# Column sums of a softmax taken through HBM and VectorE in place of products with ones, and one image's projection begun a unit sooner

## The chip, the cores and the metric

One NeuronCore of a Trainium2 chip runs the whole program. Its engines work side by side and wait for one another through semaphores: TensorE (PE, matrix products, with PEld its weight loads), VectorE (DVE), ScalarE (ACT), GpSimd (POOL) and SyncE (SP). SP and POOL also issue the DMAs, each from a queue of its own that is worked in order; 16 DMA engines carry out what both queues ask for. The time is that of the device in microseconds (us), as the median of several runs. The profile is of one execution of its own.

## What is computed

Self-attention over four images of 64 x 64 positions with 256 channels, in float32. Cut to what matters:

```python
def _L0_conv_ref(x, Wq, bq, Wk, bk, Wv, bv, gamma):
    B, W, H, C = x.shape                    # 4, 64, 64, 256
    N = W * H                               # 4096
    q = jnp.einsum('bwhc,cd->bwhd', x, Wq) + bq      # d = 128
    k = jnp.einsum('bwhc,cd->bwhd', x, Wk) + bk
    v = jnp.einsum('bwhc,cd->bwhd', x, Wv) + bv      # d = 256
    pq = q.reshape(B, -1, N)
    pk = k.reshape(B, -1, N)
    pv = v.reshape(B, -1, N)
    energy = jnp.einsum('bcn,bcm->bnm', pq, pk)
    attention = jax.nn.softmax(energy, axis=-1)
    out = jnp.einsum('bcm,bnm->bcn', pv, attention)
    out = out.reshape(B, W, H, C)
    return gamma * out + x
```

The inputs are seeded normal numbers; `gamma` is 0.5.

## The kernel before

**Tiles and units.** The energy is never stored. For each image the 4096 columns n are cut into 8 groups of 512 (`NB`), and the 4096 rows m into 16 units of 256 (two blocks of 128 rows). A unit makes exp(energy) of 256 x 512 elements as a tile `x` of 128 partitions x 2 x 512, and adds its products with `v` to four PSUM banks (`a0`, `b0`, `a1`, `b1`) that gather over the group. There are 4 x 8 x 16 = 512 units, numbered n; t = n % 16 is a unit's place in its group, and the loop over n is written out by hand (from line 706). Nothing but this order, the semaphores and the numbers of buffers sets what runs when.

**Two parts for each number.** Products run in a faster format with fewer bits, so each operand is split into an upper part `h` and two residues `l` and `d`, and each product is three products. Per unit PE does `cross` (L365, two products), `attend` for the first half of the channels (L437, six), `energy` (L380, four) and `attend` for the second half (six). `cross` and `energy` work two units ahead (`LOOK`). ACT does the exponentials (L383), the upper parts (L389) and the scaling of energies (L366). DVE does, in `halves(n + 1)`, three operations on 1024 elements for each unit: the running sum `s` (L400) and the two residues (L414, L416) into a tile `ld` with two buffers.

**The projection of the next image** (q, k, v from x) is cut into 16 steps for each pair of column blocks and slipped into the units by `step(p, engine)`: eight transposes in one step, products in six, and on DVE one or two operations of 512 elements in most (L164, L284, L309). Its results go to HBM through SP (`kf`, `qd`, `vf` stores, L337), and come back through POOL when they are needed: `load_k` in each unit, into three buffers and three units ahead; `load_q` once a group; `load_v` in the units t = 3 to 15 of an image's last group and t = 0 to 2 of the next image. The projection of image 0 runs ahead of the loop, alone.

**The column sums.** After a group, `s` (128 x 2 x 512) holds for each partition the sums over the group's units; the softmax needs the sum over all partitions and both halves, for each of the 512 columns. The kernel before does this so:

- in `halves` of the group's last unit the two halves of `s` are added (L406, `whole`);
- `sum_forms` splits the 512 columns into an upper part (ACT, L464) and a residue (DVE, L466), which are put into a `q` tile that is free at that time;
- `sums` multiplies both with a 128 x 128 matrix of ones on PE (L476), which leaves the total of each column in each partition, and ACT copies one row of it back to `s` (L477);
- `finish` is a chain of pieces, one per unit: the row goes to HBM (`zd`, L484), comes back as 128 x 4 (L486), its reciprocal is taken (L489), goes to HBM again (`rd`, L491), comes back spread over all partitions (L495), and the group's output `o` is multiplied with it (L498). Then POOL adds the input image to `o` in a DMA that accumulates (L502), and SP stores the result (L506).

`finish` begins in the unit t = 0 after the group (t = 2 in the last image), right behind `sums`. A piece runs at the end of each unit (`proceed`). The two halves of the output that were gathered in `a` and `b` are moved into `o` by `emptied` (L455, L457) at t = 15 and in the first units of the next group, and added in `finish` (L492).

The last group of all does not use `finish` but `finish_last`, which is not touched.

Of the kernel before, what the change touches and what calls it, by code (L numbers as in the profile page):

```python
# [9 lines left out]
F32 = mybir.dt.float32  # L10
F32R = mybir.dt.float32r
I32 = mybir.dt.int32
AF = mybir.ActivationFunctionType
ALU = mybir.AluOpType
AX = mybir.AxisListType
# [5 lines left out]
def kernel(  # L21
# [36 lines left out]
    nc = tc.nc  # L58
    B, W, H, C = x.shape
    P = 128  # L60
# [19 lines left out]
    UPPER = 1.0 - 2.0**-13  # L80
    REST = 1.0 / (1.0 + E)
    NB = 512
    NJ = NB // P
    NG = N // NB
    NU = NM // 2
    STEPS = NG * NU
# [4 lines left out]
    ones_r = const.tile([P, P], F32R, name="ones")  # L91
# [9 lines left out]
    with ExitStack() as fast:  # L101
        fast.enter_context(tc.manual_schedule())
        pool = lambda name, bufs, **kw: fast.enter_context(
            tc.tile_pool(name=name, bufs=bufs, **kw)
        )
        qkv = pool("qkv", 1)
        ppool = pool("ppool", 2)
        work = pool("work", 2)
        kpool = pool("kpool", 3)
        dram = pool("dram", 2, space=DRAM)  # L110
        ps_e = pool("ps_e", 2, space=PSUM)
        ps_p = pool("ps_p", 1, space=PSUM)
        ps_o = pool("ps_o", 1, space=PSUM)
# [1 line left out]

        vall = qkv.tile([P, NU, 2, 3, C], F32R, tag="v", name="v")
        wf = qkv.tile([P, 2, 3, KC, C], F32R, tag="wf", name="wf")
        zd, rd = (dram.tile([B * NG, NB], F32, tag=n, name=n, bufs=1) for n in ("zd", "rd"))
        xs4 = work.tile([P, 4, 2, XB], F32, tag="o", name="xs", bufs=1)
        raw = ppool.tile([P, 2, KC, C], F32, tag="x", name="raw")  # L120
        scaled = ppool.tile([P, 2, KC, C], F32, tag="x", name="scaled")
# [22 lines left out]
        qd, kf, vf, units, loads, now = {}, {}, {}, {}, {}, {}  # L144
        active, stores = [], []
# [49 lines left out]
        def spare(name, shape):  # L195
            pool, tag = now["banks"][now["turn"] % len(now["banks"])]
            return pool.tile(shape, F32, tag=tag, name=name)
# [142 lines left out]
        def load_v(b, t):  # L340
            for i in range(2):
                nc.gpsimd.dma_start(vall[:, t, i], vf[b, t][:, i])

        def load_q(b, g):
            loads["q", b, g] = qs[g % 2]
            nc.gpsimd.dma_start(loads["q", b, g], qd[b, g])

        def load_k(n):
# [43 lines left out]
        def halves(n):  # L392
            if n >= B * STEPS:
                return
            x, h = units[n]

            def summed():
                if n % NU:
                    s = now["s"]
                    nc.vector.tensor_tensor(s, s, x, ALU.add)  # L400
                else:
                    now["s"] = x

            def whole():
                s = now["sum"] = now["s"]
                nc.vector.tensor_tensor(s[:, 0, :], s[:, 0, :], s[:, 1, :], ALU.add)  # L406

            if n not in (1, 2):
                summed()
            if n == B * STEPS - 1:  # L410
                whole()
            ld = ppool.tile([P, 2, 2, NB], F32R, tag="ld", name=f"ld_{n}")
            l, d = ld[:, 0], ld[:, 1]
            nc.vector.tensor_tensor(l, x, h.bitcast(F32), ALU.subtract)  # L414

            nc.vector.scalar_tensor_tensor(  # L416
                d, h.bitcast(F32), 1.0 + E, x, ALU.mult, ALU.subtract
            )
            if n in (1, 2):
                summed()  # L420
            if n % NU == NU - 1 and n < B * STEPS - 1:
                whole()
            units[n] = h, l, d

        def attend(n, j, order=(0, 1, 2)):
# [30 lines left out]
                    else:  # L456
                        nc.scalar.activation(to, y, AF.Identity, scale=scale)  # L457

        def sum_forms(n):

            s = now["total"] = now["sum"]
            f = qs[n // NU % 2].rearrange("p j f a -> p (j f a)")
            h, l = now["z"] = f[:, :NB], f[:, NB : 2 * NB]
            nc.scalar.activation(h, s[:, 0, :], AF.Identity, scale=UPPER)  # L464
            yield
            nc.vector.tensor_tensor(l, s[:, 0, :], h.bitcast(F32), ALU.subtract)  # L466
            yield

        def sums(n):
            if n + NU < (B - 1) * STEPS:  # L470
                zp = spare(f"z_{n // NU}", [P, NB])
            else:
                pool, tag = (ps_o, "b1") if n // NU % 2 else now["banks"][1]
                zp = pool.tile([P, NB], F32, tag=tag, name=f"z_{n // NU}")
            for f, x in enumerate(now["z"]):
                nc.tensor.matmul(zp, ones_r, x, start=(f == 0), stop=(f == 1))  # L476
            nc.scalar.copy(now["total"][0:1, 0, :], zp[0:1, :])  # L477

        def finish(n, o, s):
            b, g = divmod(n, NG)  # L480
            r4 = rall[:, n, :]
            row = lambda t: t[n : n + 1, :]
            spread = lambda t: row(t).rearrange("o (p j) -> (o p) j", j=NJ)
            nc.sync.dma_start(row(zd), s[0:1, 0, :])  # L484
            yield
            nc.sync.dma_start(r4, spread(zd))  # L486
            yield
            yield
            nc.vector.reciprocal(r4, r4)  # L489
            yield  # L490
            nc.sync.dma_start(spread(rd), r4)  # L491
            nc.vector.tensor_tensor(o[:, 0], o[:, 0], o[:, 1], ALU.add)  # L492
            yield
            r = o[:, 1, 0]
            nc.sync.dma_start(r, rd[n, :].partition_broadcast(P))  # L495
            yield
            yield
            nc.vector.tensor_tensor(  # L498
                o[:, 0], o[:, 0], r.unsqueeze(1).to_broadcast([P, 2, NB]), ALU.mult
            )  # L500
            yield
            nc.gpsimd.dma_start(o[:, 0], xg[b, g], accum_op=ALU.add)  # L502
            yield
            yield
            yield
            nc.sync.dma_start(og[b, g], o[:, 0])  # L506

        def inside(ok, r):
# [114 lines left out]
        now["turn"], now["banks"] = 0, [(ps_p, "p0"), (ps_p, "p1")]  # L623
        rings = cycle(now["banks"]), cycle([(ps_o, tag) for tag in ("a0", "b0", "a1", "b1")])
        image(0)
        qs = [work.tile([P, NJ, 3, P], F32R, tag=f"q{g}", name=f"q{g}", bufs=1) for g in range(2)]
        loads["q", 0, 0] = qs[0]
        f3 = qs[1].rearrange("p (s w) f a -> p s w f a", s=2)
        for i in range(4):
            load_x(0, i)  # L630
        transposed(0, 0)
# [26 lines left out]
        for i in range(NI):  # L658
# [21 lines left out]
            vs = v_forms(i)  # L680
# [25 lines left out]
        for n in range(B * STEPS):  # L706
            b, u = divmod(n, STEPS)
            g, t = divmod(u, NU)
            final = n == B * STEPS - 1
            if n == 0:  # L710
                image(1)
                load_x(1, 0)
            if u == STEPS - 5 and b + 2 < B:
                image(b + 2)
            if n == B * STEPS - 6:
                xr = ppool.tile([P, 2, NB], F32, tag="s", name="xr")
                nc.sync.dma_start(xr, xg[b, g])
            cross(n + LOOK)
            turn = t == NU - 1 and not final
            if t == 0 and n:  # L720
                upper(n + LOOK - 1)
            if turn:
                zf = sum_forms(n)
                next(zf)
            p = n - 3 + (n > 6) + (n > 17)
            step(p, "act")
            late = n >= (B - 1) * STEPS
            if not final:
                attend(n, 0)
            if late and 1 <= t <= 2 and n > 1:  # L730
                emptied(n - 1 - t, 1, done, t - 1)
            energy(n + LOOK)
            load_k(n + LOOK + 3)
            store()
            if t == 0 and n:
                done = full
            if turn:
                emptied(n, 0)
            else:
                upper(n + LOOK)  # L740
            step(p, "pe")
            if t == 2 * late and n > 2:
                sums(n - 1 - 2 * late)
                active.append(finish(n // NU - 1, now["o"], now["total"]))
            if t == 0 and n and not late:
                emptied(n - 1, 1, done, vector=True)
            halves(n + 1)
            if n == 0:
                next(vs)
                next(vs, None)  # L750
            if turn:
                next(zf)
            step(p, "dve")
            if final:
                finish_last(n, xr)
                break
            attend(n, 1)
            full = now["a", 1], now["b", 1]
            if n in (6, 17):
                for engine in ("act", "pe", "dve"):  # L760
                    step(p + 1, engine)
            if t == 6 and n + NU < B * STEPS:
                load_q(*divmod(n // NU + 1, NG))
            if n >= STEPS - NU + 3 and (n - 3) // NU % NG == NG - 1 and (n - 3) // STEPS + 1 < B:
                load_v((n - 3) // STEPS + 1, (n - 3) % NU)
            proceed()

    NB = 512
    NG = N // NB
    NJ = NB // P  # L770
    NP = NM // 2
    with tc.If(nc.values_load(again[0:1, 0:1]) > 0), ExitStack() as general:
        pool = lambda name, bufs, **kw: general.enter_context(
            tc.tile_pool(name=name, bufs=bufs, **kw)
        )
        xpool, xtpool, qkv = pool("gx", 2), pool("gxt", 2), pool("gqkv", 1)
        ppool, work = pool("gp", NP + 2), pool("gw", 1)
# [13 lines left out]
        ps_o = pool("go", 1, space=PSUM)  # L791
# [72 lines left out]
        for b in range(B):  # L864
# [16 lines left out]
            for g in range(NG):  # L881
                ps = []
                mx = work.tile([P, 2, NB], F32, tag="mx", name=f"gmx_{b}_{g}")
                for t in range(NP):
                    sp = ps_s.tile([P, 2, NB], F32, tag="s", name=f"gs_{b}_{g}_{t}")
                    for h in range(2):
# [4 lines left out]
                            start=True,  # L891
                            stop=True,
# [91 lines left out]
```

## Time and profile before

| | us |
|---|---|
| median of 3 runs | 2339.01 (2337.47 to 2340.04) |
| the profiled execution's own time | 2337.63 |
| its span, first to last instruction | 2335.85 |
| mean granted TensorE clock | 0.999 of full |

| group of instructions | count | mean ns | busy us |
|---|---|---|---|
| PE products of `attend`, L437 | 6144 | 390 | 634.7, 631.9 and 631.9 for the three parts |
| PE products of the energy, L380 and L365 | 3072 | 390 | 548.2 and 316.1 |
| PE products with ones, L476 | 62 | 403 | 19.9 |
| DVE running sum, L400 | 480 | 1223 | 587.1 |
| DVE residues, L414 and L416 (without a group's first unit) | 960 | 1221 | 586.7 and 585.8 |
| DVE L406 and L466 | 32 and 31 | 685 and 684 | 21.9 and 21.2 |
| ACT L464 and L477 | 31 and 31 | 621 and 557 | 19.3 and 17.3 |

A mean is an instruction's own length in the record. Neighbouring products overlap (a product of 512 columns begins 0.227 us after the one before it), and neighbouring DVE operations by some 0.09 us, so counts times means come to more than the busy time. The DMA engines move 412.9 MB in all, 177 GB/s on the mean.

A view that tells much here is the same busy times in equal stretches. Columns: stretch and length in us, then for PE, PEld, DVE, ACT and POOL the busy us and in brackets the instructions, then the granted clock, the share of the DMA engines and GB/s. One stretch is about one group:

```profile
775.00:846.10 71.10, 71.10 (x330) 59.41 (x329) 67.02 (x67) 55.61 (x90) 9.64 (x18) 1.00 0.58 166
...
1201.60:1272.70 71.10, 71.10 (x330) 59.37 (x329) 66.66 (x68) 55.94 (x91) 18.66 (x34) 1.00 0.88 284
...
1983.70:2054.80 71.10, 71.10 (x315) 58.86 (x314) 62.86 (x58) 57.02 (x93) 10.65 (x19) 1.00 0.49 134
```

The first is an ordinary group with projection, the second one at the boundary of two images, where the next image's v is loaded, the third one of the last image, which has no projection beside it.

### The profile page before, as it was taken

How to read it: one execution, taken by the hardware profiler on the slowest of the kernel's cores; microseconds unless marked ns; L12 is line 12 of the kernel's file. 1: busy time of each engine (PE TensorE's matmuls, PEld its weight loads, DVE VectorE, ACT ScalarE, POOL GpSimd, SP SyncE). 2: the span in 40 equal slices, each digit the busy share in tenths (PEclk: the TensorE clock that was granted, in tenths of full speed). 3: DMA queues.
4: the chain of work that ended last, by engine and by line, in shares of the span. 5: the costliest groups of instructions: out<-in, count | busy, mean ns of one | idle time of the engine just before them, and what ended most of it. 6: DMA issues, size and time to landing. Idle time of an engine off the chain costs nothing.

```text
span 2335.8 us, 31727 instructions
## 1 busy us (share of the span) xinstructions
PE 2325.0 (100%) x10820; PEld 1944.9 (83%) x10820; DVE 2151.9 (92%) x2144; ACT 1829.1 (78%) x2980; POOL 416.2 (18%) x716
## 2 busy tenths in 40 slices
PE   9999999999999999999999999999999999999998
PEld 9888888888888888888888888888888888888887
DVE  8999999999999999999999999999999888888888
ACT  7778777787777877778777778777787788888886
POOL 7111111111321111111132111111113111111110
PEclk9999999999999999999999999999999999999999
DMA  8555655566985666555697556655569644444453
GB/s 271 154 173 167 183 173 152 156 174 183 297 245 152 177 177 173 164 148 171 180 326 234 144 180 168 188 159 153 167 178 342 171 135 123 122 131 114 134 134 97
DMA packets 192075, 412.90 MB, mean 177 GB/s; under 512 B 27521, under 2 KB 77443, under 8 KB 191906
## 3 DMA queue, kind: packets, MB, share of 16 engines
q0 software_dynamic: 101120, 280.54, 44.5%
q1 hardware_dynamic: 90238, 129.99, 15.9%
q8 instruction: 89, 1.46, 0.3%
q14 instruction: 80, 0.66, 0.1%
q10 hardware_dynamic: 548, 0.26, 0.0%
HBM read 305.73 MB, written 104.20 MB: 175 GB/s over the span
## 4 chain that ended last, share of the span: by engine, by line
PE 99%; DVE 1%; DMA 0%; issue 0%; ACT 0%; DVEq 0%
PE a L437 40%; PE b L437 20%; PE e L380 20%; PE e L365 10%; PE qv L256 5%; PE v L273 3%; PE xt L218 1%; PE z L476 1%; DMA xs<-in_x_dram 0%; DVE ld L414 0%; DVE ld L416 0%; DVE v L164 0%; DVE f L309 0%; DVE q L309 0%; DVE s L400 0%
## 5 line engine op out<-in xcount | busy, mean ns | idle before, releaser
L383 ACT ACTIVATE x<-e 128x512 f32<-128x512 f32 x960 | 522.0, 596 | 308.5 <-PE e L380 308.5
L400 DVE TENSOR_TENSOR s<-s,x 128x1024 f32<-128x1024 f32 x480 | 587.1, 1223 | 78.5 <-ACT x L383 76.3
L366 ACT ACTIVATE e<-e 128x512 f32<-128x512 f32 x1024 | 546.8, 572 | 132.7 <-PE e L365 132.7
L414 DVE TENSOR_TENSOR ld<-x,h 128x1024 fp32r<-128x1024 f32 x480 | 586.7, 1222 | 58.7 <-PE b L437 40.8
L437 PE MATMUL a<-h,v 128*128 128x512 f32 x2048 | 634.7, 391 | 0.0
L437 PE MATMUL b<-ld,v 128*128 128x512 f32 x2048 | 631.9, 390 | 0.6 <-DVE ld L416 0.6
L437 PE MATMUL a<-ld,v 128*128 128x512 f32 x2048 | 631.9, 390 | 0.0
L352 POOL DMA_DIRECT2D k<-kf x512 | 272.5, 532 | 1868.4 <-PE e L380 1736.3
L416 DVE SCALAR_TENSOR_TENSOR ld<-h,x 128x1024 fp32r<-128x1024 f32 x480 | 585.8, 1220 | 0.0
L380 PE MATMUL e<-q,k 128*128 128x512 f32 x2048 | 548.2, 390 | 0.0
L389 ACT ACTIVATE h<-x 128x1024 fp32r<-128x1024 f32 x480 | 510.6, 1064 | 14.2
L437 PEld LDWEIGHTS b<-ld,v 128*128 128x128 f32 x2048 | 384.4, 188 | 81.9 <-DVE ld L416 2.0
L437 PEld LDWEIGHTS a<-ld,v 128*128 128x128 f32 x2048 | 384.6, 188 | 80.9
L380 PEld LDWEIGHTS e<-q,k 128*128 128x128 f32 x2048 | 384.5, 188 | 79.5
L437 PEld LDWEIGHTS a<-h,v 128*128 128x128 f32 x2048 | 379.9, 188 | 74.9
L365 PE MATMUL e<-q,k 128*128 128x512 f32 x1024 | 316.1, 390 | 0.0
L365 PEld LDWEIGHTS e<-q,k 128*128 128x128 f32 x1024 | 192.0, 188 | 40.1
L309 DVE SCALAR_TENSOR_TENSOR f<-f,qv 128x512 fp32r<-128x512 f32 x118 | 79.5, 681 | 0.3
L256 PE MATMUL qv<-wf,xf 128*128 128x256 f32 x576 | 77.2, 285 | 0.7 <-DVE qv L284 0.4
L256 PEld LDWEIGHTS qv<-wf,xf 128*128 128x128 f32 x576 | 73.8, 191 | 3.8 <-DVE qv L284 0.6
L164 DVE SCALAR_TENSOR_TENSOR vf<-vf,v 128x512 fp32r<-128x512 f32 x96 | 65.4, 682 | 0.6 <-ACT vf L154 0.6
L414 DVE TENSOR_TENSOR ld<-s,h 128x1024 fp32r<-128x1024 f32 x32 | 39.2, 1226 | 28.7 <-ACT h L389 27.2
(95 smaller groups left out, 1166.4 us busy)
## 6 DMA issues: line engine op xcount, KB each, us to landing
k<-kf POOLq DMA_DIRECT2D x512, 384.0 KB, 3.4
vf<-vf SPq DMA_DIRECT2D x96, 384.0 KB
v<-vf POOLq DMA_DIRECT2D x96, 384.0 KB, 7.0
q<-qd POOLq DMA_DIRECT2D x31, 768.0 KB, 5.1
kf<-f SPq DMA_DIRECT2D x118, 192.0 KB
qd<-f SPq DMA_DIRECT2D x115, 192.0 KB
o<-in_x_dram POOLq DMA_DIRECT2D x31, 512.0 KB, 6.7
out_dram<-o SPq DMA_DIRECT2D x31, 512.0 KB
```

The lines of the kernel that those rows point to most:

```text
L256: nc.tensor.matmul(to[:, s, :], left, right.rearrange("p s a -> p (s a)") if w else right, start=(f == 2 and s == k == 0), stop=(f == 1 an ...
L309: nc.vector.scalar_tensor_tensor(f[:, :, :, j, :], h.bitcast(F32), s, y, ALU.mult, op)
L352: nc.gpsimd.dma_start(t, kf[b, u % NU])
L365: nc.tensor.matmul(e, *forms(n, i, 2), start=True, stop=False, skip_group_check=True)
L366: nc.scalar.mul(e, e, -REST)
L380: nc.tensor.matmul(e, *forms(n, i, f), start=False, stop=(f == 1), skip_group_check=True)
L383: nc.scalar.activation(x[:, i, :], e, AF.Exp, scale=(1.0 + E) ** 3 / E)
L389: nc.scalar.activation(h, units[n], AF.Identity, scale=UPPER)
L400: nc.vector.tensor_tensor(s, s, x, ALU.add)
L414: nc.vector.tensor_tensor(l, x, h.bitcast(F32), ALU.subtract)
L416: nc.vector.scalar_tensor_tensor(d, h.bitcast(F32), 1.0 + E, x, ALU.mult, ALU.subtract)
L437: nc.tensor.matmul(to, vall[:, t, i, f, j * P : (j + 1) * P], units[n][f][:, i, :], start=(t == 0 and i == 0 and f != 1), stop=(t == NU - ...
```

## The change

The products with ones, the split in front of them and the copy behind them go. `finish` now begins in the unit t = 15 itself. It stores both halves of `s` whole (128 x 512 each) to HBM, and eight DMAs read them back so that partition 32 j + p holds, for the 128 columns of block j, eight values of each column: from partitions p, p + 32, p + 64, p + 96 of both halves. DVE adds these eight (one reduction with 1024 inputs and 128 results), transposes the result in blocks of 32 x 32, and adds over the 32 that now lie side by side (a reduction of 128 to 4). That leaves the totals as 128 x 4, as they were before. The tile `y` that is read into takes the place of the `q` tile of the group just done; `load_q` of the group after next therefore comes at t = 8, no longer at t = 6. The pieces of `finish` now fall in the units: zd stores t = 15, y loads 0, sum of the halves of `o` 3, reductions, reciprocal and rd store 6, spread read 7, multiplication 9, accumulation 10, output store 13.

Image 1's projection begins in unit 2 instead of 3, and the unit 6 does one of its steps instead of two. In units 1 to 4 the running sum is added behind the residues, not ahead of them (before: units 1 and 2), and the last forms of image 0's v, which stood in unit 0, are made behind the residues of unit 2.

```diff
-        zd, rd = (dram.tile([B * NG, NB], F32, tag=n, name=n, bufs=1) for n in ("zd", "rd"))
+        zd = dram.tile([B * NG, 2, P, NB], F32, tag="zd", name="zd", bufs=1)
+        rd = dram.tile([B * NG, NB], F32, tag="rd", name="rd", bufs=1)
...
+        def q_tile(g, name, dtype=F32R):
+            return work.tile([P, NJ, 3, P], dtype, tag=f"q{g % 2}", name=name, bufs=1)
+
         def load_q(b, g):
-            loads["q", b, g] = qs[g % 2]
+            loads["q", b, g] = q_tile(g, f"q_{b}_{g}")
             nc.gpsimd.dma_start(loads["q", b, g], qd[b, g])
...
-            if n not in (1, 2):
+            after = 0 < n < 5
+            if not after:
                 summed()
...
-            if n in (1, 2):
+            if n == 2:
+                next(vs)
+                next(vs, None)
+            if after:
                 summed()
-            if n % NU == NU - 1 and n < B * STEPS - 1:
-                whole()
             units[n] = h, l, d
...
-        def sum_forms(n):
-            s = now["total"] = now["sum"]
-            f = qs[n // NU % 2].rearrange("p j f a -> p (j f a)")
-            h, l = now["z"] = f[:, :NB], f[:, NB : 2 * NB]
-            nc.scalar.activation(h, s[:, 0, :], AF.Identity, scale=UPPER)
-            yield
-            nc.vector.tensor_tensor(l, s[:, 0, :], h.bitcast(F32), ALU.subtract)
-            yield
-
-        def sums(n):
...
-            for f, x in enumerate(now["z"]):
-                nc.tensor.matmul(zp, ones_r, x, start=(f == 0), stop=(f == 1))
-            nc.scalar.copy(now["total"][0:1, 0, :], zp[0:1, :])
-
         def finish(n, o, s):
             b, g = divmod(n, NG)
             r4 = rall[:, n, :]
-            row = lambda t: t[n : n + 1, :]
-            spread = lambda t: row(t).rearrange("o (p j) -> (o p) j", j=NJ)
-            nc.sync.dma_start(row(zd), s[0:1, 0, :])
+            for i in range(2):
+                nc.sync.dma_start(zd[n, i], s[:, i, :])
             yield
-            nc.sync.dma_start(r4, spread(zd))
-            yield
-            yield
+            y = q_tile(n, f"y_{n}", F32).rearrange("p j f a -> p (j f) a")
+            for j in range(NJ):
+                for i in range(2):
+                    nc.sync.dma_start(
+                        y[j * 32 : (j + 1) * 32, NJ * i : NJ * (i + 1)],
+                        zd[n, i].rearrange("(a p) (j c) -> j p a c", p=32, j=NJ)[j],
+                    )
+            for _ in range(3):
+                yield
+            nc.vector.tensor_tensor(o[:, 0], o[:, 0], o[:, 1], ALU.add)
+            for _ in range(3):
+                yield
+            nc.vector.tensor_reduce(
+                y[:, 8].rearrange("p (f c) -> p c f", f=NJ),
+                y[:, :8].rearrange("p a (c f) -> p c f a", f=NJ),
+                AX.X,
+                ALU.add,
+            )
+            nc.vector.transpose(y[:, 9], y[:, 8])
+            nc.vector.tensor_reduce(r4, y[:, 9].rearrange("p (f c) -> p f c", f=NJ), AX.X, ALU.add)
             nc.vector.reciprocal(r4, r4)
-            yield
-            nc.sync.dma_start(spread(rd), r4)
-            nc.vector.tensor_tensor(o[:, 0], o[:, 0], o[:, 1], ALU.add)
+            nc.sync.dma_start(rd[n, :].rearrange("(p j) -> p j", j=NJ), r4)
             yield
...
-            p = n - 3 + (n > 6) + (n > 17)
+            p = n - 2 + (n > 17)
             step(p, "act")
...
-            if t == 2 * late and n > 2:
-                sums(n - 1 - 2 * late)
-                active.append(finish(n // NU - 1, now["o"], now["total"]))
+            if turn:
+                active.append(finish(n // NU, now["o"], now["s"]))
...
-            if n in (6, 17):
+            if n == 17:
                 for engine in ("act", "pe", "dve"):
                     step(p + 1, engine)
-            if t == 6 and n + NU < B * STEPS:
+            if t == 8 and n + NU < B * STEPS:
                 load_q(*divmod(n // NU + 1, NG))
```

## The prediction

> **What bounds the kernel now.** I read the page first: busy shares and the chain of waits.
>
> ```profile
> PE 2325.0 (100%) x10820; PEld 1944.9 (83%) x10820; DVE 2151.9 (92%) x2144; ACT 1829.1 (78%) x2980; POOL 416.2 (18%) x716
> ...
> PE 99%; DVE 1%; DMA 0%; issue 0%; ACT 0%; DVEq 0%
> ```
>
> TensorE (PE) is the chain; VectorE (DVE) is close behind. "100% busy" can hide pauses, since matmul records overlap, so I took the distance between starts from the timeline. Around the first product of ones (L476):
>
> ```profile
> 139.70 1.08 PE L380 MATMUL e<-q,k 128*128 128x512 f32 x4
> ...
> 140.61 0.64 PE L476 MATMUL z<-q,ones 128*128 128x512 f32 x2
> ...
> 141.09 0.63 PE L437 MATMUL a<-h,v 128*128 128x512 f32 x2
> ```
>
> Four L380 products fill 0.91 us (0.227 each), the pair L476 0.48, and the next product follows at once. So each L476 pair is paid in full, with no wait before it. Two places where PE does wait lie in the first units, for L416's second residue:
>
> ```profile
> 73.92 0.61 PE L437 MATMUL a<-ld,v 128*128 128x512 f32 x2
> 74.77 0.72 PE L437 MATMUL b<-ld,v 128*128 128x512 f32 x2 [0.23 <-DVE ld L416]
> ...
> 78.55 0.61 PE L437 MATMUL a<-ld,v 128*128 128x512 f32 x2
> 79.50 0.73 PE L437 MATMUL b<-ld,v 128*128 128x512 f32 x2 [0.34 <-DVE ld L416]
> ```
>
> Two products take 0.45, but here 0.85 and 0.95 pass between the starts, and about 0.1 more behind each: 1.1 us in all.
>
> Next, how much room DVE has where the new reduction goes (unit t=6 of a group), from DVE's timeline and PE's:
>
> ```profile
> 241.23 1.22 DVE L400 TENSOR_TENSOR s<-s,x 128x1024 f32<-128x1024 f32 x1
> 242.36 1.23 DVE L414 TENSOR_TENSOR ld<-x,h 128x1024 fp32r<-128x1024 f32 x1
> 243.50 1.23 DVE L416 SCALAR_TENSOR_TENSOR ld<-h,x 128x1024 fp32r<-128x1024 f32 x1
> ...
> 248.58 0.62 PE L437 MATMUL b<-ld,v 128*128 128x512 f32 x2
> ```
>
> The residue is ready at 244.73 and read at 248.58: 3.85 us of room. (1024 elements cost DVE 1.14 us from start to start.)
>
> Last, the DMA engines. Where the next image's v is loaded beside everything else (units t=3 of an image's last group to t=2 of the next image), the windows show:
>
> ```profile
> 1187.00:1191.00 4.00, 4.00 (x19) 3.29 (x18) 3.46 (x4) 2.39 (x5) 0.10 (x1) 1.00 0.84 264
> 1191.00:1195.00 4.00, 4.00 (x20) 3.30 (x19) 3.69 (x4) 3.55 (x7) 2.61 (x5) 1.00 0.82 216
> ...
> 1207.00:1211.00 4.00, 4.00 (x19) 3.34 (x18) 3.64 (x4) 3.28 (x6) 1.60 (x3) 1.00 1.12 388
> ...
> 1215.00:1219.00 4.00, 4.00 (x19) 3.31 (x18) 3.56 (x4) 3.25 (x6) 0.90 (x2) 1.00 1.14 380
> ```
>
> The last two columns are DMA share and GB/s: full from 1199 to 1239. A k load normally lands 3.4 us after its issue (page, part 6); here
>
> ```profile
> 1227.72 0.53 POOL L342 DMA_DIRECT2D v<-vf  x1 [0.39 <-DMA k<-kf]
> ...
> 1227.68 0.63 PE L365 MATMUL e<-q,k 128*128 128x512 f32 x2
> ```
>
> the k load issued at 1218.10 lands 9.34 us later, at 1227.44, and L365 reads it at 1227.68: 0.24 us of room. At the other two image boundaries (633 to 656 and 1787 to 1804) the least room, found the same way, is 1.36 and 1.38 us. Elsewhere it is 4 us and more.
>
> **The change, part by part.** Sums are against the profiled execution, 2337.63 us (span 2335.85 and 1.8 around it); the median of the runs is 2339.01, 1.4 above.
>
> (1) L476 goes, 31 pairs. Pair 0.481 (from 140.61 to 141.09), and 0.006 more for the L380 product in front, which then follows at the usual 0.227: 31 x 0.487 = -15.1 us. Nothing is put on PE.
>
> (2) Image 1's projection starts at unit 2, not 3, and the double step at unit 6 goes; the sum s is added behind the residues in units 1 to 4, and image 0's last v forms (two L164, 1.2 us) move from unit 0 to behind unit 2's residue. The late residue of unit 2 was 0.5 us late: 1.2 earlier, it is in time. Unit 3's was 0.6 late: one sum (1.14) goes from in front of it, and the eight transposes (0.9 us on PE, needed anyway) come before it. Bounds: both waits stay (0), both go (-1.1). I take -1.1.
>
> (3) Off DVE: L406 and L466, 0.69 and 0.68; off ACT: L464 and L477, 0.62 and 0.56. Both lie beside PE: 0. New on DVE: a reduction of 1024 elements, a transpose of 128x128, a reduction of 128, behind them the reciprocal. The last two have rows (L542 0.29, L489 0.17); the transpose is nearest to L510 (128x128, 0.23). The big reduction reads with a step of 512 bytes, which no row shows: at best the 1.22 of a contiguous one (L400), at worst the slowest elementwise row, POOL's L160, 1.30 for 512 elements, 2.6 for 1024. Chain: 1.9 to 3.3 us. I take 1.9, since DVE itself shows 1.22 for every 1024-element form. Room in units 7 and 8 of images 0 to 2 is 3.85, and the multiplication L498 leaves (it moves to t=9). In the last image the residue is ready 2.44 before its reader (1981.91 against 1984.35) and DVE idles 0.58 a unit: 3.0 of room. So 0; at 3.3, 8 x 0.3 = 2.4 us. Without this cover each group would pay the chain. L492 moves from t=4 to t=3: 1.14 us, one unit earlier, and the 1.4 us of room that unit 6 has today is what units 5 and 6 then have: 0.
>
> (4) DMAs on SP, per group: one row of 2 KB out and 2 KB back become 0.52 MB out (two stores) and 0.52 MB back (eight loads that wait for them). At t=15 and t=0 SP has only the vf stores and the x loads; behind the waiting loads stand one group's last vf stores at most, wanted seven units later. In ordinary groups DMA is at a share of 0.6 and k has 4 us: 0. On POOL, load_q moves from t=6 to t=8, the accumulation (L502) from t=8 to t=10; on SP the output store from t=11 to t=13, behind the x loads. At the three image boundaries this falls into the full stretch. Before the tightest k load come 0.52 MB of zd stores, and the 0.79 MB of load_q, issued at 1180.4 ahead of the slack stretch 1187 to 1195, now come at its end. At 387 GB/s that is 1.35 + 2.05 = 3.4 us; the stretch 1191 to 1195 can absorb (1 - 0.82/1.13) x 4 = 1.1. So the load is 2.3 to 3.4 us later, against room of 0.24, 1.36 and 1.38: PE waits 2.1 to 3.2, 0.9 to 2.0 and 0.9 to 2.0, 3.9 to 7.2 us in all. What is late next is the loop itself, so a wait is paid once per boundary. I take 5.5. Bounds: 0 if the queues' order favours k; with the 0.52 MB of y loads as well (1.35 x 3) and the output store late for L457 at t=15, 11.4.
>
> Sum: -15.1 - 1.1 + 5.5 = -10.7 us: 2326.9 for an execution like the profiled one, 2328.3 as a median.
>
> **The rivals.** (B) The transfers are hidden after all: -16.2, median 2322.8. For it: POOL's queue held 70% of the engines' time against SP's 43% from 1203 to 1223, so k is not starved. Against it: 0.24 us of room.
>
> (C) Slower: the strided reduction is the new bound, in each group at t=6. Decisive point: beyond 3.85 us of chain (23 finishes in images 0 to 2) and 3.0 (8 in the last) PE waits for the residue. 23 x (X - 3.85) + 8 x (X - 3.0) = 10.7 at X = 4.0, a reduction 2.7 times as long as a contiguous one; at X = 5, 42 us, 2371. For it: no row shows such a step. Against: L309 writes in runs of 128 with gaps at 0.68 for 512, no slower than contiguous forms. Since no row settles it, C gets 9%. The Trainium skill ("SBUF — State Buffer", Specifications) says that SBUF lines have 16 bytes and that each access which crosses into a new line pays a penalty; every one of the 1024 reads does so here, which speaks for C. It gives no factor for DVE, and no run so far shows one; with each read taking twice as long, an estimate, the chain would be 3.1 us.
>
> (D) A new wait at each turn: the output store, two units later and behind the x loads, still reads o when L457 wants to write it. Issued about 269.5 in the second group, wanted at 281.93: 12.4 us for 1 MB. The accumulation of the same 0.5 MB lands in 6.7. To take back 0.3 to 0.5 us in each of 31 groups it would have to need over 12 us everywhere: 9 to 15 us, median 2337 to 2343, no change. Against it: only the full stretches show landings that long (12.3 for a v load).
>
> **How the numbers follow.** No change is within 0.2%: 2334.3 to 2343.7, about what runs of this kernel can tell. Forecast 57% (its own range 2325 to 2334.5, 3% of it beyond 2334.3), B 26%, D 8%, C 9%. Faster 0.54 + 0.26 = 0.80, same 0.03 + 0.08 = 0.11, slower 0.09. Range: from B less the 1.5 us by which runs fall under their median, 2321, to the upper bounds of (4) and (3), 2322.8 + 11.4 + 2.4 = 2336.5.
>
> **What would show it.** (1) No L476 rows, the product behind L380 0.227 after it, 72.35 us per group becoming 71.86. (2) No wait of PE for L416 near 74 and 79. (3) The first reduction near 1.2 us, the transpose near 0.23, no PE wait for a residue at t=7 and 8. (4) PE gaps before L365 or L380 only near the three boundaries, 1 to 3 us each, with k landing over 10 us after issue. I am wrong if PE waits in every group (C, D), or if the boundaries show no gap (B).

## The result, and the profile after

| | before | after |
|---|---|---|
| median, us | 2339.10 (6 runs, 2337.47 to 2340.04) | 2329.38 (6 runs, 2328.59 to 2331.74) |
| the profiled execution's own time | 2337.63 | 2329.23 |
| its span | 2335.85 | 2327.4 |
| from the start of unit 0 to the start of the last product | 2262.96 | 2253.35 |

The ratio is 0.9963, 95% interval 0.9953 to 0.9974: 9.7 us less, 0.2 to 0.5%. The last row of the table, read off PE's timeline, leaves out the start-up and the end, which differ from execution to execution (unit 0 begins at 64.3 to 66.8 us in the twelve profiles of this document); it fell by 9.61 us, what the medians say too. (The span fell by only 8.45: between the last product and the end lie 8.1 us before and 9.5 after. In the three variants of the kernel before it is 8.3 to 9.3, in the seven of the changed kernel 9.1 to 9.5. So most of it can be the execution; whether the change adds to it stays open.)

The page of the changed kernel, its busy times and its chain of waits:

```profile
PE 2309.6 (99%) x10758; PEld 1931.5 (83%) x10758; DVE 2175.4 (93%) x2175; ACT 1798.7 (77%) x2918; POOL 417.3 (18%) x716
...
PE 96%; DMA 3%; DVE 0%; ACT 0%; issue 0%; POOL 0%; ACTq 0%
```

The 62 products of ones are gone and PE is still the chain, but 3% of the chain is now DMA, which had 0%. The timeline of PE where the pair L476 stood (a group's first unit; L380 is now L384, L437 is L443, L365 is L369):

```profile
138.29 1.07 PE L384 MATMUL e<-q,k 128*128 128x512 f32 x4
139.20 0.61 PE L443 MATMUL a<-h,v 128*128 128x512 f32 x2
139.65 0.62 PE L443 MATMUL a<-ld,v 128*128 128x512 f32 x2
140.10 0.62 PE L443 MATMUL b<-ld,v 128*128 128x512 f32 x2
```

Four products in 0.91, then two in 0.45 each, with nothing between. Ordinary groups take 71.81 us where they took 72.35. And where PE waited for the residue of units 2 and 3:

```profile
73.73 0.62 PE L443 MATMUL a<-ld,v 128*128 128x512 f32 x2
74.19 0.62 PE L443 MATMUL b<-ld,v 128*128 128x512 f32 x2
...
78.70 0.62 PE L443 MATMUL a<-ld,v 128*128 128x512 f32 x2
79.16 0.61 PE L443 MATMUL b<-ld,v 128*128 128x512 f32 x2
```

Start to start 0.46, no wait is noted: both are gone. VectorE's new chain, in the groups of instructions (columns: count, busy us, mean ns, idle before):

```profile
L483 DVE TENSOR_REDUCE y<-y 128x128 f32<-128x1024 f32 x31 | 61.7, 1990 | 0.0
...
L489 DVE STREAM_TRANSPOSE y<-y 128x128 f32<-128x128 f32 x31 | 9.7, 312 | 1.1
L490 DVE TENSOR_REDUCE rall<-y 128x4 f32<-128x128 f32 x31 | 8.9, 286 | 1.1
L491 DVE RECIPROCAL rall<-rall 128x4 f32<-128x4 f32 x31 | 5.5, 178 | 1.1
```

The strided reduction takes 1.98 us (the median; the mean in the row is 1.99), 1.6 times a contiguous operation of 1024 elements (1.22). PE waits for it nowhere; what PE does wait for behind the start-up is in the list of its waits (us in total, times, longest):

```profile
PE a L443 <- ACT o L463: 4.4, 2, 2.6
PE e L369 <- DMA k<-kf: 2.1, 4, 1.0
```

All of them lie at the three image boundaries. Taken from the distance between the starts of products, which counts the time around a wait too, they cost 2.9 us at the first, 2.1 and 0.5 at the second, 2.5 at the third: 8.0 us, of it 5.0 behind ACT's L463 (L457 before) and 3.0 behind k. What held L463 is one step back in its own timeline and in the chain of waits (start, us, what) around the first boundary:

```profile
641.66 0.69 ACT L463 ACTIVATE o<-a,gam 128x512 f32<-128x512 f32 x1 [3.01 <-DMA out_dram<-o]
```

```profile
616.71 10.32 DMA o<-in_x_dram
627.02 0.01 issue
627.04 14.54 DMA out_dram<-o
641.58 0.02 issue
...
641.66 0.70 ACT o L463
642.36 0.04 issue
642.40 1.20 PE a L443 x4
```

The accumulation, issued at 616.71, lands after 10.3 us (its median is 6.6; at this boundary it took 8.2 in the kernel before); only then the output store of the group before can go, and takes 14.5 us (median 5.2). ACT wants to write the same tile `o` from 638.65 on, and PE waits for ACT, which holds the bank it needs. Before, this store was issued five microseconds earlier (SP's timeline):

```profile
621.93 0.60 SPq L506 DMA_DIRECT2D out_dram<-o  x1
```

### The profile page after: what moved, and what is told of

The parts are those of the page before. It is cut to its first block, busy times and chain, and to the rows that moved or that the text cites. A ratio compares the mean times of both kernels' runs of the same rounds, so it can differ in the third digit from the quotient of the medians.

```text
span 2327.4 us, 31990 instructions
## 1 busy us (share of the span) xinstructions
PE 2309.6 (99%) x10758; PEld 1931.5 (83%) x10758; DVE 2175.4 (93%) x2175; ACT 1798.7 (77%) x2918; POOL 417.3 (18%) x716
## 4 chain that ended last, share of the span: by engine, by line
PE 96%; DMA 3%; DVE 0%; ACT 0%; issue 0%; POOL 0%; ACTq 0%
PE a L443 39%; PE e L384 19%; PE b L443 19%; PE e L369 10%; PE qv L257 5%; PE v L274 3%; DMA out_dram<-o 1%; PE xt L219 1%; DMA k<-kf 1%; DMA o<-in_x_dram 1%; DMA xs<-in_x_dram 0%; ACT qv L292 0%; ACT o L463 0%; DVE xf L165 0%; POOL v L343 0%
## 5 line engine op out<-in xcount | busy, mean ns | idle before, releaser
L443 PE MATMUL a<-h,v 128*128 128x512 f32 x2048 | 633.7, 391 | 4.4 <-ACT o L463 4.4
L443 PE MATMUL a<-ld,v 128*128 128x512 f32 x2048 | 631.1, 389 | 0.0
L443 PE MATMUL b<-ld,v 128*128 128x512 f32 x2048 | 630.6, 389 | 0.0
L384 PE MATMUL e<-q,k 128*128 128x512 f32 x2048 | 547.7, 389 | 0.0
L443 PEld LDWEIGHTS b<-ld,v 128*128 128x128 f32 x2048 | 384.2, 188 | 80.8 <-DVE ld L421 0.6
L443 PEld LDWEIGHTS a<-ld,v 128*128 128x128 f32 x2048 | 384.3, 188 | 80.6
L384 PEld LDWEIGHTS e<-q,k 128*128 128x128 f32 x2048 | 384.2, 188 | 79.8
L443 PEld LDWEIGHTS a<-h,v 128*128 128x128 f32 x2048 | 379.4, 188 | 79.4 <-ACT o L463 5.3
L369 PE MATMUL e<-q,k 128*128 128x512 f32 x1024 | 315.8, 390 | 2.1 <-DMA k<-kf 2.1
L369 PEld LDWEIGHTS e<-q,k 128*128 128x128 f32 x1024 | 191.6, 188 | 43.1 <-ACT h L393 1.4
L310 DVE SCALAR_TENSOR_TENSOR f<-f,qv 128x512 fp32r<-128x512 f32 x128 | 85.4, 678 | 0.3
```

Source lines behind the costliest of these rows:

```text
L310: nc.vector.scalar_tensor_tensor(f[:, :, :, j, :], h.bitcast(F32), s, y, ALU.mult, op)
L369: nc.tensor.matmul(e, *forms(n, i, 2), start=True, stop=False, skip_group_check=True)
L384: nc.tensor.matmul(e, *forms(n, i, f), start=False, stop=(f == 1), skip_group_check=True)
L443: nc.tensor.matmul(to, vall[:, t, i, f, j * P : (j + 1) * P], units[n][f][:, i, :], start=(t == 0 and i == 0 and f != 1), stop=(t == NU - ...
```

## The experiments

The theory after the comparison: the whole loss at the boundaries comes from transfers that share a full stretch of the DMA engines, the output store above all and k next. The rivals: the new bytes alone, the moves alone, the order in the queues, and VectorE's chain. For each run the time from the start of unit 0 to the start of the last product is given beside the median ("first to last"; before 2262.96, after 2253.35), since it shows a microsecond that the median hides. The runs come from several sessions, each with the kernel before beside it, whose median was 2337.68 to 2339.10; a ratio compares within one session, two medians of different runs may not.

**The next image's v loaded more slowly.**

```diff
-            if n >= STEPS - NU + 3 and (n - 3) // NU % NG == NG - 1 and (n - 3) // STEPS + 1 < B:
-                load_v((n - 3) // STEPS + 1, (n - 3) % NU)
+            image_now, w = divmod(n - (STEPS - NU), STEPS)
+            for i in range(NU):
+                if n >= STEPS - NU and image_now + 1 < B and w == 3 + 3 * i // 2:
+                    load_v(image_now + 1, i)
```

> The changed kernel with the next image's v loaded two tiles in three units instead of one in each (16 tiles over 24 units). Theory A: the changed kernel's 8.0 us of PE stalls at the three image boundaries (5.0 behind the output store that still reads o, 2.9 behind k) exist only because the DMA engines are full there; the v loads are 0.77 MB of a unit's about 1.74 MB (387 GB/s for 4.49 us), and taking a third of them away (15% of the stretch) lets everything land in time: stalls under 1 us, about 2321.4. Rival B: it is the burst of 1.04 MB of new stores and loads at the turn itself that delays o and k, whatever the v loads do: 3 to 6 us of stalls stay, 2324 to 2327. Rival C: the order of the queues, not the load, decides: no change, 2329.4.

Measured: 2321.45 (5 runs, 2320.88 to 2323.36), ratio to before 0.9929 (0.9916 to 0.9943); first to last 2245.20, 8.15 less than the changed kernel. No wait of PE is left behind the start-up, for o or for k: the slowest output store lands after 10.5 us instead of 14.5, the slowest k load after 8.4 instead of 11.4. The windows around the second boundary, of the changed kernel and then of this one (the last two columns are the DMA share and GB/s; before them PE, PEld, DVE, ACT, POOL and the clock):

```profile
1215.00:1219.00 4.00, 2.20 (x10) 1.50 (x8) 1.74 (x4) 1.78 (x4) 1.60 (x3) 1.00 1.12 396
...
1227.00:1231.00 4.00, 4.00 (x20) 3.29 (x19) 4.00 (x5) 2.79 (x6) 0.62 (x3) 1.00 1.14 386
1231.00:1235.00 4.00, 3.76 (x17) 2.84 (x16) 3.92 (x5) 3.15 (x6) 1.55 (x3) 1.00 1.17 375
```

```profile
1215.00:1219.00 4.00, 4.00 (x20) 3.30 (x19) 3.68 (x4) 3.97 (x7) 1.60 (x3) 1.00 1.04 366
...
1227.00:1231.00 4.00, 4.00 (x20) 3.30 (x19) 4.00 (x5) 3.55 (x7) 1.51 (x4) 1.00 0.97 298
1231.00:1235.00 4.00, 4.00 (x19) 3.34 (x18) 4.00 (x5) 3.04 (x6) 0.99 (x2) 1.00 0.94 296
```

In the changed kernel the engines run at 375 to 396 GB/s while PE stands for 1.8 of the first 4 us; with v spread out the rate falls to 366 and then to some 300, and PE is never idle. Taking a third off the rate of the v loads gave back the whole 8 us. Rivals B and C of this run fall: the burst at the turn is still there, and the order of the queues is the same but for the v loads themselves.

**The same edit in the kernel before.**

> The kernel before with the spread v loads alone. If spreading only takes away stalls that the change had made, it has nothing to take here (the kernel before shows no PE stall at the boundaries): 2338 to 2339.5, the same as before. If the full DMA stretch also cost the kernel before something unseen, it is up to some us faster, and part of the gain of the changed kernel with spread v loads would not be the change's stalls.

Measured: 2337.42 against 2337.85, ratio 0.9998 (0.9988 to 1.0008); first to last 2262.98, 0.02 from the kernel before. So spreading v has nothing to give by itself: what it gave above was the stalls that the change had made.

**Only the moves, none of the bytes.** The kernel before with the later q load, accumulation and output store. (In its last image the last output store isn't made, so that part of the output is missing; the boundaries lie ahead of that.)

```diff
-            yield
+            for _ in range(3):
+                yield
             nc.gpsimd.dma_start(o[:, 0], xg[b, g], accum_op=ALU.add)
...
-            if t == 6 and n + NU < B * STEPS:
+            if t == 8 and n + NU < B * STEPS:
```

> The kernel before with only the moves: q load at t=8 instead of 6, accumulation and output store two units later; none of the new bytes. If the moves make the stalls, 4 us or more of PE stalls appear at the boundaries, for o or k: 2343 or more. If the new bytes are needed as well (1.04 MB, 2.7 us at 387 GB/s, against an output store that was 2.8 to 3 us late), under 2 us: 2339 to 2341.

Measured: 2341.90 (10 runs, 2340.76 to 2344.84), ratio 1.0015 (1.0005 to 1.0024); first to last 2267.20, 4.2 more than before. PE's stalls at the boundaries come to 4.2 us by the distance between starts, 2.6 behind ACT's L457 and 1.6 behind k. Its list of waits, which leaves out the time around a wait, has less:

```profile
PE a L437 <- ACT o L457: 2.0, 2, 1.7
...
PE e L365 <- DMA k<-kf: 0.8, 3, 0.3
```

Between the two expectations in time, within the first in stalls: the moves alone, with no new byte, already make ACT wait for the output store.

**Only the bytes, none of the moves** (dummy copies `zx`, `zy` on SP in the kernel before).

```diff
+        def extra(n):
+            for i in range(2):
+                nc.sync.dma_start(zx[n, i], xg[divmod(n, NG)][:, i])
+            yield
+            for j in range(NJ):
+                for i in range(2):
+                    nc.sync.dma_start(
+                        zy[n, j * 32 : (j + 1) * 32, NJ * i : NJ * (i + 1)],
+                        zx[n, i].rearrange("(a p) (j c) -> j p a c", p=32, j=NJ)[j],
+                    )
...
+            if turn:
+                active.append(extra(n // NU))
```

> The kernel before with only the new bytes, as a dummy: at t=15 two copies of 256 KB and at t=0 eight of 64 KB on SP's queue, of the sizes and row lengths of the changed kernel's stores and loads but from HBM to HBM, and nothing waits for them. The moves alone gave 3.8 us of PE stalls at the boundaries, moves and bytes together 8.0. If bytes alone do as much and the two only add up: about 4 us, 2343. If each alone is mostly absorbed and it is the sum that passes the room: 2 us or less, 2339 to 2341. If the bytes are the cause of nearly all (the moves' 3.8 being counted in it): 7 us or more, 2346.

Measured: 2350.62 (2350.41 to 2350.86), ratio 1.0052 (1.0035 to 1.0069); first to last 2274.92, 12 more than before. But none of it for o or k. DVE's timeline in the first group of image 1:

```profile
660.57 0.68 DVE L166 SCALAR_TENSOR_TENSOR xf<-xf,xt 128x512 fp32r<-128x512 f32 x1
667.66 0.18 DVE L502 RECIPROCAL rall<-rall 128x4 f32<-128x4 f32 x1 [6.42 <-DMA rall<-zd]
667.76 1.21 DVE L402 TENSOR_TENSOR s<-s,x 128x1024 f32<-128x1024 f32 x1
```

The row of sums, a DMA of 2 KB that this kernel still sends out and back, now stands on SP behind the eight dummy loads, which wait for their stores; the reciprocal waits for the row, everything behind it on DVE waits too, and PE stands still for 3.5 us, twice; nearly all of the other 5 us are products behind these two pauses, at a granted clock of 0.50 to 0.62. My "nothing waits for them" was wrong: whatever follows in the queue does. As a measure of the bytes alone the run fails, and its wait does not occur in the changed kernel, whose row of sums is not sent at that point. It says one thing for the question: with the accumulation and the store at their old place the bytes alone made PE wait neither for o nor for k. (At the first two boundaries the pause may have covered k loads; at the third there is no pause, and no wait for k either.)

**Half of the bytes.** DVE adds the halves of `s` first.

```diff
+            if n % NU == NU - 1 and n < B * STEPS - 1:
+                whole()
...
-            for i in range(2):
-                nc.sync.dma_start(zd[n, i], s[:, i, :])
+            nc.sync.dma_start(zd[n, 0], s[:, 0, :])
...
-                y[:, :8].rearrange("p a (c f) -> p c f a", f=NJ),
+                y[:, :4].rearrange("p a (c f) -> p c f a", f=NJ),
```

(and four read-backs for eight.)

> The changed kernel, but DVE adds the two halves of s first (31 additions of 512, beside PE), and only that half goes through HBM: 0.26 MB out and back instead of 0.52, and the strided reduction has 512 elements. If the new bytes make the boundary stalls, half of them (0.52 MB, 1.35 us at 387 GB/s) comes off each late landing: stalls 8.0 to about 4 us, 2325.4. If it is the later place of the q load, accumulation and output store, stalls stay at 7 to 8 us and the time near 2329. The shorter reduction (about 1.0 instead of 1.98 us) changes no time if it is hidden.

Measured: 2327.38 (4 runs, 2326.21 to 2328.97), ratio to before 0.9953 (0.9938 to 0.9968); first to last 2251.19. The stalls come to 2.0, 1.2 and 1.0 us, 4.2 in all, as expected of the bytes, and 1.6 us are paid for the clock (see the last section), which is why first to last fell by 2.2 and not by 3.8. So both count: moves alone 4.2, moves with half the bytes 4.2, moves with all the bytes 8.0, and no wait for o or k from the bytes alone. They do not add up in proportion: the first half of the bytes cost nothing on top of the moves, the second half 3.8; why was not tested.

**The row of reciprocals read back one unit sooner.**

```diff
             nc.sync.dma_start(rd[n, :].rearrange("(p j) -> p j", j=NJ), r4)
-            yield
             r = o[:, 1, 0]
...
-            if t == 8 and n + NU < B * STEPS:
+            if t == 7 and n + NU < B * STEPS:
```

> The changed kernel with the row of reciprocals read back one unit sooner, so that the multiplication, the accumulation and the output store come at t=8, 9 and 12 instead of 9, 10 and 13, and the next q load at t=7 instead of 8 (v loads as in the changed kernel). Theory A: the waits of ACT for the output store at the first two boundaries (5.0 us of PE) go, since that store starts 4.5 us sooner and was 2.8 to 3 us late; the k waits at the third stay: about 2324.4. Rival: in a full stretch bytes sent sooner only push others back, and k waits take their place: stalls stay near 8 us, 2329.4.

Measured: 2338.67 (11 runs, 2335.13 to 2342.90), ratio 1.0000 (0.9991 to 1.0009): the whole gain is lost. Both expectations fail, and for one reason that neither held. The waits for the output store are gone and the boundary stalls fall to 2.4 us, the number of theory A but not its waits (see below), and in most groups DVE (first line, DVE's timeline; then PE's) now waits:

```profile
180.41 1.22 DVE L497 TENSOR_TENSOR o<-o 128x1024 f32<-128x1024 f32 x1 [0.88 <-DMA o<-rd]
```

```profile
184.17 0.64 PE L443 MATMUL a<-ld,v 128*128 128x512 f32 x2
185.10 0.73 PE L443 MATMUL b<-ld,v 128*128 128x512 f32 x2 [0.29 <-DVE ld L421]
```

The row, issued at 174.19, landed 6.2 us later; the multiplication stood at the head of DVE for 0.9 us (25.5 us over 26 groups), and the residues behind it came late for PE. The unit that I took away looked empty, and was the time of a DMA. The 2.4 us at the boundaries are no waits for k. At each of the three, ACT waits for a store of q that still reads the tile `f`, and PE then waits 0.7 to 0.9 us for ACT's exponentials:

```profile
ACT vf L155 <- DMA qd<-f: 7.0, 3, 2.4
```

The first of these stores was issued at 623.67 and took 9.1 us: a third kind of transfer that holds a tile too long there.

**The same, with the chain itself one unit sooner**, so that the row keeps its time. For that the reduction is made shorter by three additions, first alone:

```diff
-            nc.vector.tensor_reduce(
+            nc.vector.tensor_tensor(y[:, 8:12], y[:, :4], y[:, 4:8], ALU.add)
+            nc.vector.tensor_tensor(y[:, :2], y[:, 8:10], y[:, 10:12], ALU.add)
+            nc.vector.tensor_tensor(
                 y[:, 8].rearrange("p (f c) -> p c f", f=NJ),
-                y[:, :8].rearrange("p a (c f) -> p c f a", f=NJ),
-                AX.X,
+                y[:, 0].rearrange("p (c f) -> p c f", f=NJ),
+                y[:, 1].rearrange("p (c f) -> p c f", f=NJ),
                 ALU.add,
             )
```

> The changed kernel with the eight rows of blocks added by three contiguous additions (512, 256 and 128 elements; the last one also does the reordering) in place of the one strided reduction of 1024. From rows of 1.22 us for 1024, about 0.7 for 512 and 0.3 for 128, the three take 1.1 to 1.3 us from start to start against 1.98, so the least room of the residue grows from 1.17 and 0.31 to about 1.9 and 1.0 us. If the chain is hidden, as I hold, the time stays at 2329.4; if it takes part in the time, 0.7 x 31 = 22 us less.

Measured: 2330.69 (5 runs, 2327.59 to 2331.75), ratio to before 0.9964 (0.9950 to 0.9979), as the changed kernel; first to last 2253.13 against 2253.35. The three took 1.6 us from start to start, more than I had estimated, so the least room grew only to 1.59 and 0.76. The chain is hidden: 0.4 us less of it, 31 times, changed nothing. Then with `for _ in range(2)` in place of 3 ahead of the additions and the q load at t = 7:

> The tree version with VectorE's chain one unit sooner, at t=5 (multiplication t=8, accumulation 9, output store 12, next q load t=7), v loads as in the changed kernel. It is the repair that the run with the earlier read-back missed: there the multiplication came before the row of reciprocals (it landed 6.6 us after issue) and VectorE waited; here the row keeps its full time. Theory A (the late output store makes ACT and PE wait at the first two boundaries): these waits go, about 2.4 us of boundary stalls are left as in that run, 2324 to 2325.5. The chain's 2.5 us stands against 2.5 us of room in unit 7: if that is just too little, PE waits some 0.3 us in each of 23 groups, 7 us, and it is 2331 or more. If bytes sent sooner only push k back: about 2329.

Measured: 2327.92 (5 runs, 2325.61 to 2328.63), ratio to before 0.9956 (0.9942 to 0.9971); first to last 2250.15, 3.0 less than the tree at t = 6. PE's waits behind the start-up:

```profile
PE e L369 <- DMA k<-kf: 1.6, 4, 0.8
...
PE e L369 <- ACT h L393: 0.5, 1, 0.5
```

No wait for o is left, and the room in unit 7 was just enough (0.17 us; groups with projection grow by up to 0.03, the second one by 0.3). Of the boundary stalls 3.9 us stay by the distance between starts (1.8, 0.6 and 1.5), all in front of the product that reads k, and not the 2.4 that I took over from the run above, which were no waits for k: at the first boundary, where k was in time in the changed kernel, PE now waits 1.8 us. The pause for the store had covered those loads. The median lies between the 2324 to 2325.5 of theory A and the 2329 of k pushed back; the gain is less sure in it than in the trace.

**The reduction twice.**

```diff
-            nc.vector.tensor_reduce(
+            for _ in range(2):
+                nc.vector.tensor_reduce(
```

> The changed kernel with the strided reduction run twice into the same place: VectorE's chain at t=6 grows by 1.98 us. The trace of the changed kernel leaves 1.17 us for the residue in unit 8 of images 0 to 2 and 0.31 us in the last image. If these are the rooms, PE waits 23 x (1.98 - 1.17) + 8 x (1.98 - 0.31) = 32 us: 2361. If VectorE has other slack (its idle time in the units around), 0 to 10 us: 2329 to 2339. If later units inherit the delay, over 45 us.

Measured: 2372.01 (4 runs, 2370.47 to 2372.29), ratio to before 1.0142 (1.0125 to 1.0159); first to last 2296.27, 43 more than the changed kernel. PE's waits:

```profile
PE b L443 <- DVE ld L421: 12.5, 31, 0.4
PE a L443 <- DVE ld L419: 7.9, 9, 0.9
PE a L443 <- ACT o L463: 4.8, 2, 2.9
```

Once in each of the 31 groups, in unit 8, as the rooms say, and not in later units. A group grows by 1.07 us in images 0 to 2 and by 1.92 in the last one, 0.25 more than 0.81 and 1.67: the pair took 4.04 rather than 3.96, and a product behind a wait starts about 0.11 late. 23 x 1.07 + 8 x 1.92 = 40 us; the other 3 are some 15 products at half the clock after two boundary pauses. So the rooms of 1.17 and 0.31 us are real, and VectorE has no other slack for the chain.

**The old start.**

```diff
-            after = 0 < n < 5
+            after = n in (1, 2)
...
-            if n == 2:
-                next(vs)
-                next(vs, None)
...
-            p = n - 2 + (n > 17)
+            p = n - 3 + (n > 6) + (n > 17)
```

(with the two v forms back in unit 0 and the double step at unit 6.)

> The changed kernel with the old start: image 1's projection from unit 3, the double step at unit 6, the sum ahead of the residues again outside units 1 and 2, and the last v forms in unit 0. If the two start-up waits of PE (0.85 and 0.95 between starts that take 0.45) belong to this order, they come back: 1.1 us more, 2330.5, and the rest of the trace is the same. If the lighter work of units 2 and 3 took them away, 0: 2329.4.

Measured: 2332.89 (10 runs, 2330.89 to 2334.52), ratio to before 0.9976 (0.9966 to 0.9985). Both waits are back, and units 0 to 16 take 73.10 us for 71.86: 1.2 us, as in the kernel before. (The run undoes the earlier start, the order of the sum and the place of the v forms together; which of them removes the waits was not separated.) The medians, of two sessions, differ by 3.5; first to last by 2.7. Of these, 1.2 us are a slower clock after the first boundary's pause in the profiled execution, and the start-up ahead of unit 0 was about 2 us longer in it than in the changed kernel's. What remains between medians beyond 1.2 is open.

## Why the prediction was right, and where it was off

The forecast was 2328.3 and the time is 2329.38, by the mechanism that it named: the products' time comes off, and waits at the three boundaries take part of it back. That the total is only 1 us off is partly luck, since steps (1) and (4) miss by 1.4 and 2.5 us in opposite directions. Step by step, by the time from unit 0 to the last product, -9.6 us:

| step | predicted | measured |
|---|---|---|
| (1) L476 goes | -15.1 | -16.5 |
| (2) the start-up waits | -1.1 | -1.2 |
| (3) VectorE's chain | 0 | 0 |
| (4) transfers at the boundaries | +5.5 | +8.0 |
| sum | -10.7 | -9.7 (-9.6 taken directly) |

(1) Mis-sized by 1.4 us. The group became 0.53 us shorter (72.347 to 71.813; predicted 71.86). The term took the pair itself and the product in front, 0.487. The nine products behind the pair had also run a little slower than 0.227 each (0.231 to 0.236 for most), 0.043 us together, and do so no longer.

(2) As predicted; with the old start the waits return.

(3) Zero, but with much less to spare than the step says. It took 1.9 us for the chain, on the ground that VectorE shows 1.22 for every form of 1024 elements; the reduction takes 1.98 and the chain 2.9. The rooms of 3.85 and 3.0 shrank to 1.17 in units 8 of images 0 to 2 and to 0.31 in those of the last image. Rival C needed a chain 4.0 long to take the gain back, and gave 2371 for one of 5; the run with the reduction twice, a chain of 4.9, took 2372, with 3 us of it for the clock. The Trainium skill ("SBUF — State Buffer", Specifications), which was set beside C, says that crossing into a new 16-byte line costs something: the row agrees, with 1.6 times, though no run separates the step from the reduction as such.

(4) The sum was low by 2.5 us, and its make-up was wrong, which is the failed step. It gave all of the 5.5 us to k, 1 to 3 us at each boundary and most at the second, and left "the output store late for L457 at t=15" to the upper bound. That store made 5.0 us, at the first two boundaries, and k 3.0: nothing at the first, 0.5 at the second, 2.5 at the third. The store's path had been lengthened twice, by its later place and by an accumulation that itself lands later (10.3 us for 8.2 at the first boundary); I worked out how late k would be by adding the bytes ahead of it, but did not do the same for the store. Rival D had the right wait and the wrong place: it asked for that wait in every group, where it would need 12 us, and not at the two boundaries where the store took 14.5 and 13.4 (at the third it took 7.9). Rival B failed only by the boundaries: with v spread out, first to last is 17.8 us below the kernel before, where B had 16.2, and 1.4 of the difference is what (1) was short of.

The version with spread v loads is the best: 17 us less than before, where the change alone gave 9.7.

## What to carry to other kernels

A change that frees the busiest engine by moving bytes has to be costed where the DMA engines are already full, and there for each buffer that a transfer still holds, not for the loads alone: list the stores that must be done before a tile is written again, add up their path, and compare with the time of the next writer. When such a stretch turns out to be the loss, look first for the transfer in it that has no hurry; here loading v over 24 units and not 16 gave back all 8 us. And a gap between two steps that shows no work may be the latency of a DMA: before it is closed, look at what lands in it.

## What the runs showed of the hardware that was not expected

The granted clock can halve after a short pause of PE. With half of the bytes, PE waited 1.8 us (by the profile) for ACT, ran six products at full speed, and then (columns as above; the clock is the third from the end):

```profile
641.00:642.00 1.00, 0.63 (x3) 0.54 (x4) 1.00 (x2) 1.00 (x3) 0.00 (x0) 1.00 1.10 396
642.00:643.00 1.00, 1.00 (x6) 0.82 (x5) 1.00 (x2) 1.00 (x3) 0.00 (x0) 0.94 1.10 398
643.00:644.00 1.00, 1.00 (x4) 0.81 (x3) 0.34 (x2) 0.90 (x2) 0.00 (x0) 0.50 1.14 398
```

The clock is 0.50 from about 643 to 646; each product takes 0.427 us and not 0.227, 1.6 us in all. In the changed kernel's profiled execution pauses of 2.8 and 2.0 us (by the distance between starts) were followed by full speed (1.00 throughout), with the reduction twice pauses of 3.1 and 2.0 us by half speed; with the old start a pause of 2.7 us was followed by half speed, with the tree one of 2.2 us was not. So the same pause can cost 1.2 to 1.6 us more or nothing, and the times of the changed kernel (3.2 us between the fastest and the slowest of six) may owe some of their spread to it, as to the start-up; that was not tested. The Trainium skill ("TensorE: Matmul & The Clock Gate", Part 1) puts the fall to half speed after at least one idle window of about 3.4 us; here it came after a pause of 1.8 to 1.9 us, so pauses shorter than that are not safe.

A reduction in VectorE that reads with a step of 512 bytes takes 1.07 us for 512 inputs and 1.98 for 1024, 1.8 ns for each further one, where contiguous elementwise operations take 0.68 and 1.22, 1.05 ns. That the step makes the difference is likely and not shown: no run reduces 1024 contiguous inputs, but the contiguous reduction of 128 (L490, 0.29 us) takes no longer than an elementwise operation of 128 (L510, 0.29).
